# Ordering attention keys beside the scores instead of ahead of them, in blocks of 16 heads

## Chip, core and metric

The kernel runs on one NeuronCore of a Trainium2 chip. The metric is the device time of one execution in microseconds: 10973.53 us, the median of 3 runs (10972.97 to 10985.72). A core has five engines with queues of their own: TensorE (PE in the profile, PEld for its weight loads), VectorE (DVE), ScalarE (ACT), GpSimd (POOL) and SyncE (SP). SP and POOL issue the transfers (DMAs) between HBM and SBUF. Each engine works through its own list in order. An instruction that waits holds up all that stand behind it in that list.

## What is computed

Four layers over a graph of 3327 nodes with 128 features and a dense matrix `adj`; each layer adds its result to `x`. The change concerns the first, an attention with 128 heads of 8 elements each:

```python
q = (x @ Wq.T).reshape(d, n, h)      # d = 128 heads, n = 3327, h = 8
k = (x @ Wk.T).reshape(d, n, h)
v = (x @ Wv.T).reshape(d, n, h)
a = jnp.einsum('dnh,dmh->dnm', q, k) * scale
a = a + spatial_encoding + edge_encoding          # both are adj
a = jax.nn.softmax(a, axis=2)
out = jnp.einsum('dnm,dmh->dnh', a, v)
```

Here `x` is the input after a normalisation and a ReLU. The reshape reads the flat products in a new order: one head is a run of 3327 x 8 numbers of the flat product, so its keys must be put in a new order before they are of use. The three later layers multiply by `adj` or its transpose and are not touched.

## The kernel before, in words

**Preparation (L326 to L436).** Nodes are held as 26 tiles of up to 128. For each pair of tiles PE projects keys and queries. The keys go to HBM as they are (`kraw_d`, one long row per element, in which head d has N numbers from d * N on). Queries are split into a high part, rounded to fp32r, and the rest (`qS_d`). Between them the first four "squares" of `adj` are transposed: `Square` (L264) loads 32 rows at a time as `rows`, DVE turns them in two halves into `cols` (L288) and takes the largest of each row (L292); `store` writes `cols` to `adjT` in pieces of 512 bytes; `gather`, `back` and `finish` take the row maxima through HBM as 4-byte elements, into `bound_d`, the shift of the exponent. Then 13 steps project the values, two tiles each, and store them through two buffers (L427 to L436). In the last eight of these steps `k_halves(e)` (L412) orders the keys of one element for all 128 heads: it loads a row per head from `kraw_d`, splits it into high part (ACT, L420) and rest (DVE, L421), even and odd tiles apart, and makes four stores to `kS_d`. The order of the instructions in the preparation is left to the scheduler of the framework. Behind it stand two branches: a slow path that these inputs don't take (L458), and the main one (L599).

**Attention (L599 to L831).** From here the order is written out by hand. Target nodes go in 7 chunks of 476 columns, in each of them 32 groups of 4 heads, in each group 13 pairs of source tiles. All pairs are numbered through as u. For each pair and head PE adds q.k onto a PSUM bank that DVE has seeded with adj minus the shift (`seed`, L642), ACT takes the exponent (L666, L669), for some banks DVE by a polynomial (`hand_exp`, L685), and PE multiplies by the values into `po` (L713). At the end of a group DVE copies `po` to `OS` (L721), and POOL stores it to `oT_d` (L725).

`loads(u)` (L727) prepares the next group while one is worked on. With q the pair's place in its group: at q = 1 SP issues `load_k` (16 transfers of `KT` from `kS_d`), the first `load_q` and `load_v`; at q = 3, 5, 7 POOL negates the queries just loaded (`negate_q`, L570) and SP issues the next `load_q`, which waits for that negation because both write the same tile; at q = 8 POOL spreads the values (`spread_v`, L580) and copies one column of `KT` to `seen` (`all_here`, L584). The first scores of the next group wait for `seen`.

`plan(u, f)` (L755) puts other work behind pair u: it is issued at that place in every engine's list, ahead of the pair's `loads`. `plan_squares(c)` (L758) spreads the squares of the next chunk over this one: one square over four groups, its rows loaded at a group's first pair, turned at the fifth and tenth, their largest taken at the thirteenth; `gather` stands at the first pair of the fifth group, `back` at its second, `finish` and `store` at its eighth and ninth. The pool `e_t` has one buffer for `rows` and one for `cols`, so a new load waits until the old contents have been used.

```python
            if at == 0 and i >= 0:
                for f, a in behind.pop(i // 4, ()):
                    f(*a)
            if at == 0 and 0 <= i // 4 < n:
                loads(i // 4)
```

## Time and profile before

| what | us |
|---|---|
| median of 3 runs | 10973.53 |
| the profiled execution, its own time | 10981.99 |
| its span, first to last instruction | 10980.2 |
| last eviction of the values ends | 351.4 |
| last subtraction of the keys (DVE, L421) ends | 413.85 |
| first scores | 456.16 |
| `OS` copies of group 0 and of group 32 | 511.55 and 1897.46 |
| PE busy, share of the span | 10536.5, 96% |
| ACT busy | 10031.9, 91% |
| DVE busy | 8481.1, 77% |
| POOL busy | 1532.1, 14% |

The profile is of one execution. In timelines each line has the start in us from the span's beginning, the duration (of all instructions merged in the line), engine, line of the kernel, operation, what it writes and reads, how many, and in brackets how long the engine was idle before and what released it. In the list of waits a line says who waited for whom, for how long in total, how often, and the longest. A busy share of PE counts pipelined matmuls and is no measure of its peak.

### The profile page before, as it was taken

The numbers are of one execution on the slowest core, as the hardware profiler recorded it, in microseconds if no ns is written. First come the engines' busy times: TensorE is split into PE (matmuls) and PEld (weight loads), VectorE is DVE, ScalarE is ACT, GpSimd is POOL, SyncE is SP. The second block draws the span as 40 slices with busy tenths as digits, with TensorE's granted clock in tenths as the row PEclk, the third lists the DMA queues.
The fourth block names the chain that finished last, engine by engine and source line by source line (L and its number), as shares of the span: only waits on it lengthen the run. The fifth ranks groups of instructions, "written<-read, shape, count | busy, mean of one in ns | idle before, by whom it ended". The sixth has DMA issues, their size and how long they took to land. (4 is left out here: it accounts for less than half of the span.)

```text
span 10980.2 us, 204468 instructions
## 1 busy us (share of the span) xinstructions
PE 10536.5 (96%) x72876; PEld 3438.3 (31%) x72876; DVE 8481.1 (77%) x13503; ACT 10031.9 (91%) x13789; POOL 1532.1 (14%) x2480
## 2 busy tenths in 40 slices
PE   4599999999999999999999999999999999999889
PEld 2133333333333333333333323333323333333544
DVE  5588887888878887788887888878877777777655
ACT  3599999999999999999999999999999999999330
POOL 5011111111111111111111111111111111111101
PEclk7799999999999999999999999999999999999999
DMA  8865665665565565565556555565555555554678
GB/s 249 254 99 94 96 96 111 96 97 95 89 119 94 96 97 86 109 99 93 90 95 118 94 96 93 94 118 97 87 92 96 97 94 87 81 88 72 203 235 281
DMA packets 695338, 1256.97 MB, mean 114 GB/s; under 512 B 195218, under 2 KB 555049, under 8 KB 691244
## 3 DMA queue, kind: packets, MB, share of 16 engines
q1 hardware_dynamic: 644044, 1114.42, 55.4%
q0 software_dynamic: 50272, 129.37, 4.3%
q8 instruction: 586, 9.60, 0.4%
q14 instruction: 436, 3.57, 0.1%
HBM read 1096.53 MB, written 146.60 MB: 113 GB/s over the span
## 5 line engine op out<-in xcount | busy, mean ns | idle before, releaser
L666 ACT ACTIVATE e<-S 128x952 f32<-128x952 f32 (+1 forms) x9024 | 8366.0, 1102 | 40.3 <-PE S L654 33.6
L713 PE MATMUL po<-e,VA 128*9 128x476 f32 (+1 forms) x46592 | 5739.3, 565 | 33.1 <-DVE OS L721 12.6
L645 DVE TENSOR_TENSOR S<-a,shb 128x476 f32<-128x476 f32 (+1 forms) x5824 | 3940.7, 677 | 1450.4 <-ACT e L666 1062.5
L654 PE MATMUL S<-QS,KT 64*128 64x476 f32 (+1 forms) x22176 | 4533.8, 445 | 77.8 <-DMA a<-adjT 23.3
L654 PEld LDWEIGHTS S<-QS,KT 64*128 64x128 f32 x22176 | 2077.0, 184 | 5103.7 <-ACT e L666 1281.6
L669 ACT ACTIVATE e<-S 128x476 f32<-128x476 f32 (+1 forms) x4128 | 2476.1, 714 | 24.1 <-PE S L654 23.6
L695 DVE SCALAR_TENSOR_TENSOR e<-e,h 128x476 f32<-128x476 f32 (+1 forms) x2240 | 1493.9, 667 | 77.0
L713 PEld LDWEIGHTS po<-e,VA 128*9 128x9 f32 x46592 | 691.0, 88 | 1606.3 <-issue 1487.9
L570 POOL TENSOR_SCALAR QS<-QS 128x476 fp32r<-128x476 f32 (+1 forms) x669 | 484.8, 725 | 4292.9 <-DMA QS<-qS_d 2457.6
L725 POOL DMA_DIRECT2D oT_d<-OS x896 | 471.9, 532 | 3665.3 <-DVE OS L721 3622.1
L691 DVE TENSOR_SCALAR h<-S 128x476 f32<-128x476 f32 (+1 forms) x1120 | 728.0, 650 | 327.0 <-PE S L654 322.5
L697 DVE SCALAR_TENSOR_TENSOR e<-e,EA 128x476 f32<-128x476 f32 (+1 forms) x1120 | 754.0, 673 | 0.0
L695 DVE SCALAR_TENSOR_TENSOR e<-h 128x476 f32<-128x476 f32 (+1 forms) x1120 | 743.6, 664 | 0.0
L1110 PE MATMUL pu<-strip,y 128*128 128x512 f32 (+2 forms) x1456 | 600.2, 566 | 30.3 <-DVE y L971 14.8
L654 PE MATMUL S<-QZ,KT 64*128 64x476 f32 (+1 forms) x1120 | 494.4, 441 | 10.6 <-DVE S L645 9.3
L1110 PEld LDWEIGHTS pu<-strip,y 128*128 128x128 f32 (+1 forms) x1456 | 271.4, 191 | 304.5 <-issue 271.1
L580 POOL COPY VA<-VR 128x832 f32<-128x832 f32 x224 | 245.6, 1097 | 24.7 <-DMA VR<-v_d 24.7
L1114 DVE TENSOR_REDUCE deg<-strip 128x1 f32<-128x1536 f32 (+1 forms) x104 | 193.7, 1881 | 62.1 <-DMA strip<-adjT 43.5
L654 PEld LDWEIGHTS S<-QZ,KT 64*128 64x128 f32 x1120 | 205.4, 183 | 87.1 <-DVE S L645 47.7
L288 DVE STREAM_TRANSPOSE cols<-rows 128x416 f32<-128x416 f32 x208 | 204.5, 988 | 30.6 <-DMA rows<-in_adj_dram 23.4
L721 DVE COPY OS<-po 128x476 f32<-128x476 f32 (+1 forms) x224 | 146.2, 653 | 88.8 <-PE po L713 88.8
L1063 ACT COPY uT<-pu 128x512 f32<-128x512 f32 (+1 forms) x21 | 11.1, 553 | 222.3 <-PE pu L1110 222.3
(256 smaller groups left out, 1956.7 us busy)
## 6 DMA issues: line engine op xcount, KB each, us to landing
KT<-kS_d SPq DMA_DIRECT2D x1792, 208.0 KB
KT<-kS_d SPq DMA_DIRECT2D x1792, 104.0 KB
VR<-v_d SPq DMA_DIRECT2D x224, 416.0 KB
QS<-qS_d SPq DMA_DIRECT2D x3072, 14.9 KB
QS<-qS_d SPq DMA_DIRECT2D x1536, 29.8 KB
adjT<-cols SPq DMA_DIRECT2D x26, 1664.0 KB
a<-adjT SPq DMA_DIRECT2D x156, 238.0 KB
strip<-adjT POOLq DMA_DIRECT2D x39, 895.5 KB, 5.5
```

The source lines that it names most:

```text
L570: nc.gpsimd.tensor_scalar(QS[b][:, j + 1, :w], QS[b][:, j, :w].bitcast(F32), -1.0, 0.0, op0=ALU.mult, op1=ALU.add)
L580: nc.gpsimd.tensor_copy(VA[(c * NG + g) % 2][:, :, :, 0:H], v.rearrange("p j (t e) -> p t j e", e=H))
L645: touch(u, [r], nc.vector.tensor_tensor(bank(u, r), adj_of[c][2 * q + r][:, :w], shift_of[c][:, :w], op=ALU.subtract))
L654: x = nc.tensor.matmul(bank(u, r), KT[b][64 * r:64 * r + 64, max(0, j - 1), q * P:(q + 1) * P], q_s[64 * r:64 * r + 64, :w], start=hand an ...
L666: touch(u, (0, 1), nc.scalar.activation(e[:, :, :w], S[:, odd:even + 1, :w], AF.Exp, scale=2.0))
L669: touch(u, [r], nc.scalar.activation(e[:, 1 - r, :w], bank(u, r), AF.Exp, scale=2.0))
L691: touch(u, [1], nc.vector.tensor_scalar(s, bank(u, 1), EXP_ARG, None, op0=ALU.mult))
L695: nc.vector.scalar_tensor_tensor(e, s if k == 3 else e, EXP_C[k], s, op0=ALU.add, op1=ALU.mult)
L697: nc.vector.scalar_tensor_tensor(e, e, EXP_C[0], EA[pairs[u][2]][:, :w], op0=ALU.add, op1=ALU.mult)
L713: nc.tensor.matmul(po[32 * j:32 * j + H + 1, :w], VA[k % 2][:, 2 * pairs[v][2] + of, j, :], e_of[v, j][:, 1 - of, :w], start=(q == 0 and r ...
L725: nc.gpsimd.dma_start(oT_d[:, d * N + c * CW:d * N + c * CW + w], o[32 * j:32 * j + H + 1, :w])
L1110: nc.tensor.matmul(ps[:, :k], y[:m, t, :], s[:m, c * 4 * P - c0:c * 4 * P - c0 + k], start=(t == 0), stop=(t == NT - 1))
```

## The change

`k_halves` becomes `k_block(b)`: the 128 partitions now hold 16 heads with 8 elements each instead of 128 heads of one element (`KB` is 16), so eight blocks replace eight elements. Only block 0, of the heads that the first four groups use, is ordered in the preparation, at the third step of the values. Blocks 1 to 7 are planned into the first chunk, each over 52 pairs (four groups), ahead of the four groups that use it.

A block loads its rows at its pair 0 into the `cols` buffer. `high` is a DVE copy of 6 or 7 tiles into the `rows` buffer, stored by SP; `low` is a POOL subtraction in the same buffer, in place, so it waits for the high part's store, and is stored in its turn. There are four such high and low pairs, at 8 and 10, 14 and 17, 23 and 25, 27 and 31. The block's keys are first loaded at pair 40.

Chunk 0 no longer calls `plan_squares`. Its four squares go into blocks 1 to 4, behind the keys: a tighter timetable in pairs 32 to 52, with `gather` and `store` at pair 52, the next block's pair 0, and `back` and `finish` at 58 and 64. The `rows` buffer grows from 832 to 896 columns. The slow path orders blocks 1 to 7 itself. The same numbers are computed as before.

```diff
+KB = P // H
-            self.rows = self.pool.tile([P, KW], F32, name="rows")
+            self.rows = self.pool.tile([P, 7 * P], F32, name="rows")[:, :KW]
+    def k_rows(b):
+        return bass.AP(tensor=kraw_d.tensor, offset=kraw_d.offset + KB * b * N, ap=[[N, KB], [GP, H], [1, N]])
+    def k_store(b, i, r, q0, half):
+        m = half.shape[-1]
+        nc.sync.dma_start(bass.AP(
+            tensor=kS_d.tensor, offset=kS_d.offset + (i * H * HEADS + KB * b) * NP + (r * NQ + q0) * P,
+            ap=[[NP, KB], [HEADS * NP, H], [1, m]]), half)
+    def k_block(b, pool):
...
-            if t0 >= 10:
-                k_halves(t0 // 2 - 5)
+            if t0 == 4:
+                k_block(0, a2)
...
-                if c + 1 < NC and (g, q) == (0, 0):
+                if c and c + 1 < NC and (g, q) == (0, 0):
                     plan_squares(c)
...
+                def load(self):
+                    raw = e_t.tile([P, NT, P], F32, name="cols").rearrange("p t n -> p (t n)")
+                    nc.gpsimd.memset(raw[:, N:NP], 0.0)
+                    nc.sync.dma_start(raw[:, :N], k_rows(self.b))
+                    self.of = raw.rearrange("d (p q r) -> d r q p", q=NQ, r=2)
+                def high(self, r, q0, q1):
+                    self.part = e_t.tile([P, 7 * P], F32, name="rows")[:, :(q1 - q0) * P]
+                    nc.vector.tensor_copy(self.part.rearrange("d (q p) -> d q p", p=P).bitcast(F32R),
+                                          self.of[:, r, q0:q1, :])
+                    k_store(self.b, 0, r, q0, self.part)
+                def low(self, r, q0, q1):
+                    part = self.part.rearrange("d (q p) -> d q p", p=P)
+                    nc.gpsimd.tensor_tensor(part.bitcast(F32R), self.of[:, r, q0:q1, :], part, op=ALU.subtract)
+                    k_store(self.b, 1, r, q0, self.part)
+            def plan_keys():
+                for b in range(1, HEADS // KB):
+                    u, keys = 4 * (b - 1) * NQ, Keys(b)
+                    plan(u, keys.load)
+                    for hi, lo, r, h in ((8, 10, 0, 0), (14, 17, 0, 1), (23, 25, 1, 0), (27, 31, 1, 1)):
+                        plan(u + hi, keys.high, r, 7 * h, 7 + 6 * h)
+                        plan(u + lo, keys.low, r, 7 * h, 7 + 6 * h)
+                    if b <= squares_of(1) - squares_of(0):
+                        sq = Square(e_t, squares_of(0) + b - 1)
+                        for j, (t0, t1, t2) in enumerate(((32, 36, 37), (38, 40, 41), (42, 48, 49), (49, 51, 52))):
+                            plan(u + t0, sq.load, j)
+                            plan(u + t1, sq.turn, j, 0)
+                            plan(u + t2, sq.turn, j, 1)
+                            plan(u + t2, sq.largest, j)
+                        for k, f in ((52, sq.gather), (52, sq.store), (58, sq.back), (64, sq.finish)):
+                            plan(u + k, f)
+            plan_keys()
```

More of the change, by code (lines that the diff above doesn't have):

```diff
@@ L320, in square @@
         return q
+    def k_rows(b):
[6 more added lines that the diff above has]
+    def k_block(b, pool):
+        raw = pool.tile([P, NP], F32, name="st_q0")
+        nc.gpsimd.memset(raw[:, N:NP], 0.0)
+        nc.sync.dma_start(raw[:, :N], k_rows(b))
+        of = raw.rearrange("d (p q r) -> d r q p", q=NQ, r=2)
+        for r in range(2):
+            hi = pool.tile([P, NQ, P], F32R, name="st_k0")
+            lo = pool.tile([P, NQ, P], F32R, name="st_q1")
+            nc.scalar.copy(hi, of[:, r])
+            nc.vector.tensor_tensor(lo, of[:, r], hi.bitcast(F32), op=ALU.subtract)
+            for i, half in enumerate((hi, lo)):
+                k_store(b, i, r, 0, half.bitcast(F32).rearrange("d q p -> d (q p)"))
     def head_rows(tensor):
@@ L410, in bound_scores @@
             return wide
-        def k_halves(e):
-            raw = a2.tile([P, NP], F32, name="st_q0")
-            nc.gpsimd.memset(raw[:, N:NP], 0.0)
-            nc.sync.dma_start(raw[:, :N], head_rows(kraw_d[e]))
-            of = raw.rearrange("d (p q r) -> d r q p", q=NQ, r=2)
-            for r in range(2):
-                hi = a2.tile([P, NQ, P], F32R, name="st_k0")
-                lo = a2.tile([P, NQ, P], F32R, name="st_q1")
-                nc.scalar.copy(hi, of[:, r])
-                nc.vector.tensor_tensor(lo, of[:, r], hi.bitcast(F32), op=ALU.subtract)
-                for i, half in enumerate((hi, lo)):
-                    nc.sync.dma_start(kS_d[i, e, :, r * NQ * P:(r + 1) * NQ * P],
-                                      half.bitcast(F32).rearrange("d q p -> d (q p)"))
         v_rows = v_d.rearrange("(p t) d -> p t d", t=NT)
@@ L460, in gnn_kernel @@
                 square(d2, s, d2)
+            for b in range(1, HEADS // KB):
+                k_block(b, d1)
             for t in range(NT):
@@ L756, in plan, with __init__ @@
                 behind.setdefault(u, []).append((f, a))
+            class Keys:
+                def __init__(self, b):
+                    self.b = b
+                def load(self):
+                    raw = e_t.tile([P, NT, P], F32, name="cols").rearrange("p t n -> p (t n)")
+                    nc.gpsimd.memset(raw[:, N:NP], 0.0)
+                    nc.sync.dma_start(raw[:, :N], k_rows(self.b))
[10 more added lines that the diff above has]
+            def plan_keys():
+                for b in range(1, HEADS // KB):
+                    u, keys = 4 * (b - 1) * NQ, Keys(b)
[12 more added lines that the diff above has]
+                            plan(u + k, f)
             def plan_squares(c):
```

## The prediction

> **What bounds the kernel now.** I read the page's slices first, for where TensorE is not full.
>
> ```profile
> PE   4599999999999999999999999999999999999889
> ACT  3599999999999999999999999999999999999330
> DMA  8865665665565565565556555565555555554678
> ```
>
> Each digit is 274.5 us. Two slices at the start have PE at 4 and 5 with DMA at 8: the preparation. Then PE and ACT stand at 9 with DMA at 5 or 6. So the start is bound by transfers, the middle by PE and ACT together. Second view: windows (columns: stretch, its length, busy us and instructions of PE, PEld, DVE, ACT, POOL, then clock, DMA share, GB/s).
>
> ```profile
> 260.00:415.00 155.00, 57.98 (x131) 25.83 (x131) 78.81 (x62) 67.01 (x43) 7.53 (x19) 0.71 0.92 352
> ...
> 460.00:1860.00 1400.00, 1385.71 (x10041) 424.83 (x10044) 1133.41 (x1744) 1395.36 (x1903) 187.01 (x304) 1.00 0.61 102
> ...
> 141.00:146.00 5.00, 4.55 (x6) 1.99 (x7) 1.50 (x3) 2.07 (x4) 4.34 (x7) 0.52 0.98 289
> ...
> 763.00:776.00 13.00, 12.71 (x94) 3.59 (x93) 11.18 (x18) 12.84 (x18) 2.11 (x4) 1.00 0.99 124
> ```
>
> 260 to 415 us is the values' projection with all eight `k_halves`: DMA is 92% busy, PE a third. 460 to 1860 is the first chunk: DVE has a fifth of its time free and DMA two fifths. The last two lines give prices: storing a square (512-byte pieces) runs at 289 GB/s, so 1664 KB take 5.9 us; loading a group's `KT` (16 copies of each row) runs at only 124 GB/s, so 8 x 208 + 8 x 104 KB take 20.6 us.
>
> Third view: one plain group's loads on POOL and on the SP queue, in order of time.
>
> ```profile
> 784.13 1.08 POOL L570 TENSOR_SCALAR QS<-QS 128x476 fp32r<-128x476 f32 x1 [10.21 <-DMA QS<-qS_d]
> 788.93 0.83 POOL L570 TENSOR_SCALAR QS<-QS 128x476 fp32r<-128x476 f32 x1 [3.72 <-DMA QS<-qS_d]
> 793.56 0.59 POOL L570 TENSOR_SCALAR QS<-QS 128x476 fp32r<-128x476 f32 x1 [3.80 <-PE S L654]
> ...
> 795.34 0.18 POOL L584 COPY seen<-KT 128x3 f32<-128x3 f32 x1
> ```
>
> ```profile
> 673.27 1.75 SPq L299 DMA_DIRECT2D rowmax_d<-rm  x4
> 682.18 0.38 SPq L304 DMA_DIRECT2D four<-rowmax_d  x1
> 682.97 1.35 SPq L551 DMA_DIRECT2D KT<-kS_d  x3
> ...
> 803.17 1.70 SPq L551 DMA_DIRECT2D KT<-kS_d  x4
> ```
>
> A group takes 43.2 us (the `OS` copies stand at 814.02 and 857.24), a pair 3.32. A group's `OS` copy is issued 16 pairs behind its first scores, so those of the group with `OS` at 857.24 came at 804.1; call such a time F. The next group's `KT` is issued at F - 1 (803.17), as soon as the buffer is free. `KT` issue to `seen` took 35.4 us (760.06 to 795.5): 20 us of data, then three rounds of load, negate, load. So `seen` stands at F + 34.5 and the next scores at F + 43.2: the spare time is 8.7 us. The SP lines show how it can go: the 4-byte writes of `gather` took 8.9 us until `four` could be read behind them, `KT` was issued at 682.97 (F + 8.5), `seen` ended at 716.6 and the next F was 717.8. Fourth view, waits: what a late transfer costs.
>
> ```profile
> DVE cols L288 <- DMA rows<-in_adj_dram: 8.9, 1, 8.9
> ...
> PE S L654 <- POOL seen L584: 5.8, 2, 4.3
> ```
>
> The one DVE wait of 8.9 us made its group 53.1 us (`OS` at 8183.34 and 8236.41), 9.9 longer; the PE wait of 4.3 made one 49.3 (5145.21 and 5194.52), 6.1 longer. DVE and PE have no reserve against a late tile beyond a pair or so.
>
> **What the preparation gains.** Seven of eight key loads and 28 of 32 key stores go: 7 x (1664 + 4 x 832) KB = 35.8 MB, at 352 GB/s 102 us if nothing else bound. But the projection stays: 13 steps of two tiles, each 4 evictions and a 1024 KB store. Before, the last eviction (ACT 350.29, 1.07 us) ended at 351.4 and the rest to 413.9 was keys alone: 62.5 us, the lower bound. Up to 351 the steps waited on the store two back (38.8 us of DVE idle there). The third step was at 291.5, held by the first stores beside keys and 4-byte `bound_d` writes; that stays. The other ten took 6.0 us each; PE needs 3.7 (8 records at 0.668 us overlap to 3.70 in the timeline), upper bound 84 us. I take 4.3, since the store's round trip over two buffers stays in the loop: 291.5 + 43 + 1.3 = 336, **78 us** gained. The start-up behind it (414 to first scores at 456) stays.
>
> **What the first chunk pays.** New prices. `high` reads with a stride of 26 elements: L421 reads the same stride at 3333 / 1664 = 2.0 ns per element, L390 contiguously at 1954 / 3328 = 0.59; I take the strided row, 1.5 us for 6 tiles and 1.8 for 7 (low end 0.5). `low`: POOL's two-input add took 1269 / 512 = 2.5 ns, so 1.9 to 2.2 us; strided up to twice that. A 384 or 448 KB store takes 1.2 us at 374 GB/s (the keys' rate at 399 to 412) and I allow 3 us from issue to landing; from 1 (a `QS` load's last issue to its negation) to 8.9 (`gather`). `behind` work of pair p reaches DVE at F + 3.32p + 1.4 (a plain square's `largest` at p = 12: F + 41.1). Seven blocks of four groups A to D:
>
> 1. A, blocks 2 to 5: the square before ends at p = 0. Its last turn and `largest` end at F + 3.4, `gather` issues to 5.2, the store of `cols` follows and needs 5.9 us, behind the 4-byte writes or beside them: landed at F + 12 to 18, I take 15. `Keys.load` uses the same buffer, so SP waits there, and the group's `KT` behind it. 1.7 MB at 374 GB/s come first (4.5 us), so `KT` data start near F + 20 and `seen`, 33 us later, is near F + 53: 10 us late, 11 us paid. Four times: **44** (24 to 60). A DVE wait in the same place (`finish` at p = 12, whose `four` is queued behind those loads) lies beside this.
> 2. B, the same blocks: the high store (p = 8) is queued behind the late `load_q`, the low follows it, and high at p = 14 waits for the row buffer: 3 us x 4 = **12** (0 to 20).
> 3. B, all blocks: at p = 14 SP waits for the copy before it issues `KT`, so `KT` leaves at F + 7 instead of F - 1; `seen` comes 33.6 us later (682.97 to 716.6), F + 41, just in time. But low (p = 17) stands behind `negate_q` and its store behind `load_q`; it lands at F + 36 to 37, high at p = 23 is due at F + 34.6: 2 us x 7 = **14** (0 to 20).
> 4. C, blocks 1 to 4: `KT` leaves at F + 7 again (p = 27), low (p = 31) runs after the first negation at F + 29 (22 us behind `KT`, as 682.97 to 704.89 in the group above), its store lands at 36, only then may the rows of the square (p = 32) come, behind `load_q`: issued 37 to 39, landed 41. The turn at p = 36 is due at F + 34.6: 6.5 us x 4, at the price above **26** (0 to 40).
> 5. The first raw load, 4.5 us, stands ahead of group 1's `KT`, whose `seen` was already late: **4** (0 to 5).
> 6. Inserted work: 28 copies, 28 subtractions and denser turns. DVE is free 0.6 us of each 3.3, a copy takes 1.8; groups with three 1 us operations of a square are at most 0.1 us longer than plain ones. I take 0.4 per copy with its subtraction: **11** (1 to 42).
>
> POOL's subtraction can also hold DVE: at 714.72 the final multiply (L697) took 1.03 us instead of 0.65 while POOL's `VA` copy ran from 715.19; that is in item 6 at its row's price, 0.4. The Trainium skill (SBUF — State Buffer, Who interferes with whom) says a VectorE instruction with two SBUF inputs and a GpSimd instruction that reads SBUF exclude each other for a whole instruction; seeds have two such inputs. By that rule 28 subtractions of about 2.06 us could hold seeds for 58 us, where the row gives 11.
>
> Sum: 44 + 12 + 14 + 26 + 4 + 11 = 111 against 78: **33 us slower**. The profiled execution took 10981.99 us (span 10980.2 and 1.8 around it), 8.5 over the median 10973.53; 11015 by its own clock, 11006.5 beside the median, so 11006.
>
> **Rivals.**
> - It hides (faster): stores of keys and squares land soon enough that items 2 to 4 vanish and item 1 pays 6 us a time. For it: DMA is 39% idle in the chunk, and the SP lines show a square's `gather` wait used up without loss. Against: the order of the SP queue, not bandwidth, sets my delays. It decides where the waits come to under 78 us, a `cols` store landing by F + 12. Price 24 + 4 + 11 = 39, so 39 us faster, 10935; with the gain at 84 and less inserted, 10905.
> - Near balance: half of items 2 to 4 (26) with 44 + 4 + 11 = 85: 10980.
> - The dependence is coarse: `k_store` and `load_k` interleave in one DRAM tensor. If SP waits for each store's landing before the next `KT`, that is 3 us more in B and C of seven blocks, 42 us: 11048. Nothing in this trace has a load of `kS_d` between its stores, so neither way is shown.
> - The preparation doesn't shrink as said: the steps stay at 6 us, the gain 62.5: 11022. Against: the key stores beside them are gone.
>
> **Chances.** Forecast 0.43; coarse 0.10; preparation 0.07; balance 0.17; hidden 0.23. Range 10930 to 11080: hidden beyond 39 us and sums with item 1 at 60 and item 4 at 40 fall outside. Its own range for the forecast: 10996 to 11045. A measurement tells 0.2%, 22 us, from no change: slower 0.58 (forecast, coarse, most of preparation), same 0.19, faster 0.23.
>
> **What would show it.** The projection should end near 336 and first scores near 378. In the waits: PE on `seen` some 10 us four times, ahead of groups 5, 9, 13 and 17; DVE on `rows` in four groups for 6 us; high on its buffer for 2 to 3. Groups of plain chunks must stay at 43.2. If the `OS` copies of the first chunk stay at 43.2 to 44 us throughout, items 1 to 4 are wrong; if the first scores come after 395, the gain is.

## The result, and the profile after

| | us |
|---|---|
| before, median of 4 runs | 10978.91 (10972.97 to 10985.72) |
| after, median of 4 runs | 11112.02 (11105.01 to 11113.34) |
| ratio after to before | 1.0119, 95% interval 1.0106 to 1.0131 |

The change makes the kernel 133 us slower; the forecast was 33 us slower. The two profiled executions differ by 129.5 us in span, and it goes by stretches like this. OS(n) is the start of the copy of group n's output, L733 in after and L721 in before.

| stretch | before | after | difference | forecast |
|---|---|---|---|---|
| start to first scores | 456.2 | 376.3 | -79.8 | -78 |
| first scores to OS(0) | 55.4 | 67.4 | +12.1 | +4 |
| OS(0) to OS(32), first chunk | 1385.9 | 1594.4 | +208.5 | +107 |
| OS(32) to OS(223) | 8275.3 | 8261.6 | -13.7 | 0 |
| rest of the span | 807.5 | 809.8 | +2.4 | 0 |
| sum | 10980.2 | 11109.7 | +129.5 | +33 |

Of the 13.7 us by which the later chunks are shorter, 6.8 lie in the one chunk where before had the late group with PE's wait of 4.3 us; after is not late there. The rest is spread over the other chunks.

The page's slices of after, the same three rows as of before:

```profile
PE   4788899999999999999999999999999999999889
ACT  3587899999999999999999999999999999999430
DMA  8766565656556555565655556565555555554678
```

The second slice rises from 5 to 7, since the preparation ends 80 us earlier. The next three fall from 9 to 8 on PE: that is the first chunk with the keys in it. From the sixth on PE's row is the same. The windows of after (stretch, length, busy us of PE, PEld, DVE, ACT, POOL, then clock, DMA share, GB/s) show the same two places:

```profile
260.00:336.00 76.00, 57.97 (x131) 26.64 (x131) 33.66 (x48) 20.94 (x29) 6.40 (x12) 0.81 0.76 240
443.00:2038.00 1595.00, 1430.99 (x9988) 426.96 (x9984) 1184.46 (x1751) 1391.91 (x1883) 250.81 (x338) 0.94 0.61 108
```

The projection now fits into 260 to 336 us (it ended near 336, as forecast); DMA is busy for 76% of that time, where it was for 92% of 260 to 415 us. In the first chunk PE ran the same work, but its granted clock is 0.94 on average, where before had 1.00. That column had no step in the prediction.

The group differences OS(n) - OS(n-1), against a plain group of 43.2 us:

| groups | excess in after, us | sum | forecast |
|---|---|---|---|
| A behind a square (4, 8, 12, 16) | 27.3, 26.5, 25.3, 25.3 | 104 | 56 (items 1, 2) |
| B (1, 5, ... 25) | 5.3 to 7.7, mean 6.5 | 46 | 14 (item 3) |
| C with a square's turns (2, 6, 10, 14) | 11.1, 10.1, 10.7, 11.7 | 44 | 26 (item 4) |
| A without a square (20, 24) | 3.7, 4.9 | 9 | 0 |
| D (3, 7, 11, 15) | 1.5 each | 6 | 0 |

So 194 of the 209 us stand where the prediction put them, and there they are 1.7 to 3.3 times as large; 15 stand in groups for which it had nothing. (The forecasts of the table are 96 us; the 11 of item 6 were spread over all groups.) Now to what the losses are made of. The waits of the first chunk in after (who <- for whom: total us, times, longest):

```profile
POOL cols L777 <- DMA adjT<-cols: 95.6, 4, 24.3
...
DVE rows L783 <- DMA kS_d<-rows: 54.5, 12, 8.7
DVE b L309 <- DMA four<-rowmax_d: 52.0, 4, 15.4
PE S L666 <- POOL seen L596: 50.2, 5, 14.5
...
DVE cols L289 <- DMA rows<-in_adj_dram: 25.5, 4, 6.5
```

First line: GpSimd at the fill of `cols` ahead of a raw load; it waits for the store of the square's columns. Second: the high half waits for its row buffer, 12 times. Third and fourth: `finish` on its row maxima and PE on the marked keys, in four blocks, at the same time (the fifth wait of PE is another group's). Last: the turns of the squares, 6.4 us four times. The forecast had 10, 3 (and 2) and 6.5 us for these. The SP queue in block 2's A group (first scores near 582.4; start, duration):

```profile
585.88 1.75 SPq L300 DMA_DIRECT2D rowmax_d<-rm  x4
587.68 0.58 SPq L296 DMA_DIRECT2D adjT<-cols  x1
599.63 0.56 SPq L778 DMA_DIRECT2D cols<-kraw_d  x1
600.29 11.92 SPq L563 DMA_DIRECT2D KT<-kS_d  x10
```

The queue stands from 588.3 to 599.6 for the columns' store, then the raw load goes, and only behind it the next group's keys: item 1's mechanism, 17.2 us behind the first scores where 15 were taken. What it costs is seen in windows along the end of this group:

```profile
614.00:627.50 13.50, 12.89 (x95) 3.87 (x95) 8.82 (x14) 12.38 (x18) 0.00 (x0) 1.00 1.03 130
627.50:642.00 14.50, 0.04 (x4) 0.00 (x0) 1.12 (x3) 1.23 (x2) 3.18 (x5) 0.60 0.34 64
642.00:650.00 8.00, 7.92 (x44) 2.37 (x48) 6.52 (x7) 5.11 (x7) 2.64 (x2) 0.66 0.28 67
650.00:653.00 3.00, 3.00 (x23) 0.85 (x15) 0.30 (x1) 3.00 (x6) 0.00 (x0) 1.00 0.61 153
653.00:661.00 8.00, 0.06 (x1) 0.00 (x0) 3.24 (x5) 0.95 (x2) 0.00 (x0) 0.79 0.15 25
661.00:670.00 9.00, 8.98 (x57) 2.46 (x57) 5.95 (x10) 6.71 (x9) 2.13 (x4) 0.81 1.05 163
```

PE stands 14.5 us for `seen`, then works at a clock of 0.66: 44 matmuls in 8 us where the first line has 95 in 13.5. Then it stands 8 us more, while the second high half waits for its buffer (7.4 us by the timeline), and works again at 0.81. Two stands of 22.5 us together and some 4.4 us of work lost at half clock make nearly all of the 27.3.

This adds up over the whole chunk. PE's stands of more than 0.3 us between OS(0) and OS(32) are 153.4 us in after (2.4 in before). The trace's record of the granted clock has 21 stretches at 0.5 that begin in this time, in steps of 3.4 us (3.4 to 17.1), 177.5 us in all; before has none. Half of the part of them that lies outside of the stands is 52.0 us of lost work. 153.4 + 52.0 = 205.4 of the 208.5. **A quarter of the loss is the clock behind the waits, not the waits.** This reckoning says where PE's time went; what made PE stand, it does not say. The Trainium skill (TensorE: Matmul & The Clock Gate, Part 1: The HAM clock gate) says the array falls to half rate after an idle window of about 3.4 us and needs one busy window to come back. The steps of 3.4 us agree. But here shorter stands were followed by half clock as well: all those of 2.4 us or more, such as the 2.8 us from 691.1 to 693.9, and three of the nine of 1.2 to 1.9 us (at 907.6, 1047.1 and 1655.0).

One row stands behind a size that was wrong. The raw load of block 2 in after:

```profile
601.50:608.50 7.00, 7.00 (x56) 2.44 (x52) 5.95 (x10) 7.00 (x10) 0.87 (x2) 1.00 0.98 215
```

and a raw load of one element in before:

```profile
362.00:369.50 7.50, 0.00 (x0) 0.00 (x0) 0.00 (x0) 3.11 (x1) 0.00 (x0) 0.50 1.00 426
```

The same 1.7 MB, the same packets of 13308 bytes, and the DMA engines fully busy in both, but 215 instead of 426 GB/s. A packet takes 1000 ns instead of 498 (medians of the 128 packets of such a load), so the load takes 8 us instead of the 4.5 that I took from before.

### The profile page after: what moved, and what is told of

The parts are those of the page before. It is cut to its first block, busy times and chain, and to the rows that moved or that the text cites. A ratio compares the mean times of both kernels' runs of the same rounds, so it can differ in the third digit from the quotient of the medians.

```text
span 11109.7 us, 204547 instructions
## 1 busy us (share of the span) xinstructions
PE 10591.1 (95%) x72876; PEld 3448.5 (31%) x72876; DVE 8496.4 (76%) x13517; ACT 9995.8 (90%) x13775; POOL 1597.6 (14%) x2508
## 5 line engine op out<-in xcount | busy, mean ns | idle before, releaser
L1163 PE MATMUL pu<-strip,y 128*128 128x512 f32 (+2 forms) x1456 | 599.8, 566 | 30.7 <-DVE y L1024 14.8
L733 DVE COPY OS<-po 128x476 f32<-128x476 f32 (+1 forms) x224 | 146.4, 653 | 96.9 <-PE po L725 96.9
L1116 ACT COPY uT<-pu 128x512 f32<-128x512 f32 (+1 forms) x21 | 11.1, 554 | 222.1 <-PE pu L1163 222.1
```

Of the source, the lines that this page charges most:

```text
L1163: nc.tensor.matmul(ps[:, :k], y[:m, t, :], s[:m, c * 4 * P - c0:c * 4 * P - c0 + k], start=(t == 0), stop=(t == NT - 1))
```

## The experiments

**Theory 1** is the prediction's: the order on SP's queue and the single buffers `cols` and `rows` set the delays. **Theory 2**: the engines hold each other up (GpSimd's subtraction and VectorE share a way to SBUF; more operations). **Theory 3**: the loads of keys depend coarsely on the stores. The trace of after already speaks against it, in two lines of SP's queue:

```profile
658.60 0.54 SPq L329 DMA_DIRECT2D kS_d<-rows  x1
659.24 13.54 SPq L563 DMA_DIRECT2D KT<-kS_d  x16
```

The load of keys is issued 0.1 us after the issue of the store has ended, its first packet (661.43) starts before the store's last one ends (661.82), and nowhere in the chunk does SP's own list of waits have a load of `KT` that waits for a store.

All runs, beside runs of before on the same chip; "stretch" is OS(0) to OS(32) less the 1385.9 of before, "stands" and "clock" are its two parts, worked out as above.

| kernel | time, us | ratio, 95% | first scores | stretch | stands | clock |
|---|---|---|---|---|---|---|
| after | 11112.0 | 1.0106 to 1.0131 | 376.3 | 208.5 | 153.4 | 52.0 |
| finish moved | 11100.1 | 1.0091 to 1.0125 | 374.0 | 196.6 | 137.4 | 58.1 |
| two row buffers | 11066.0 | 1.0060 to 1.0093 | 373.6 | 168.3 | 119.8 | 44.2 |
| no read by GpSimd | 11104.7 | 1.0094 to 1.0128 | 374.7 | 209.5 | 160.4 | 51.4 |
| raw behind keys | 11063.2 | 1.0063 to 1.0094 | 373.6 | 170.4 | 128.5 | 45.3 |
| GpSimd's queue | 11082.7 | 1.0088 to 1.0119 | 372.7 | 175.1 | 127.2 | 44.6 |
| rows by element | 11223.0 | 1.0200 to 1.0234 | 399.7 | 281.0 | 212.8 | 70.5 |
| other pitch | 11117.0 | 1.0111 to 1.0142 | 375.1 | 207.8 | 155.5 | 48.7 |
| eight transfers | 11111.2 | 1.0111 to 1.0142 | 374.9 | 204.2 | 147.1 | 55.7 |
| layout alone | 11012.5 | 1.0022 to 1.0049 | 493.6 | -1.4 | 1.9 | 0 |
| squares in preparation | 11142.4 | 1.0135 to 1.0166 | 526.9 | 84.9 | 52.0 | 30.3 |
| pieces | 11113.0 | 1.0110 to 1.0141 | 524.2 | 62.2 | 45.9 | 16.9 |
| pieces, rows by element | 11142.1 | 1.0141 to 1.0169 | 548.3 | 63.3 | 50.0 | 12.9 |
| new plan, GpSimd | 11061.3 | 1.0057 to 1.0085 | 376.2 | 160.8 | 121.4 | 45.5 |
| new plan, its queue | 11055.6 | 1.0056 to 1.0084 | 376.1 | 136.1 | 88.2 | 44.5 |
| new plan, VectorE | 10992.2 | 1.0004 to 1.0022 | 374.4 | 73.2 | 54.4 | 6.3 |
| new plan, finer | 10990.2 | 1.0000 to 1.0018 | 377.5 | 87.8 | 68.3 | 10.7 |

### What in the order costs how much

**The bounds' writes moved away.**

```diff
-for k, f in ((52, sq.gather), (52, sq.store), (58, sq.back), (64, sq.finish)):
+for k, f in ((52, sq.gather), (52, sq.store)):
+    ...
+plan(16 * NQ + 32 + b, sq.back)
+plan(16 * NQ + 36 + b, sq.finish)
```

> Kernel after, but the last two steps of the four squares of the second chunk (reading the row sums back, and writing the bounds of four bytes each) are planned for a late group of the first chunk, away from the blocks of keys. Theory 1 (the order on the one queue and the single buffers): the second high half of blocks 2 to 5 no longer waits behind the small writes, so its wait falls from 7.4-8.7 us to about 3 in four blocks, about 20 us: some 11092 us. The wait of PE for the negations after each block (14.5 us, four times) stays, since only the finish that lay beside it has gone. Theory 2 (engines hold each other up): the same work is done in another place, so 11112 within 6 us. Theory 3 (dependence of the loads of keys on the stores): 11112 within 6 us, too.

Measured: 11100.1. Its waits in the first chunk:

```profile
DVE rows L783 <- DMA kS_d<-rows: 34.4, 13, 3.5
...
PE S L666 <- POOL seen L596: 45.3, 4, 12.5
...
DVE b L309 <- DMA four<-rowmax_d: 2.3, 2, 1.5
```

The second high half's wait fell from 7.4-8.7 to at most 3.5, and `finish` waits no more, while PE's wait for `seen` stays: `finish` did lie beside it, as item 1 said, and the bounds' write made the 4 to 5 us that item 2 lacked. The trace of after shows how: in block 2 the low half's store had moved its last packet at 652.34, and 13 of its 16 completions came by 652.8, but the last came at 657.57, among those of the bounds' write that was issued behind it at 649.78. In this run the same copy starts 0.5 us behind the store's last packet. The four A groups lost 23.6 us; groups B and others gave half of it back, so 12 us came out of the 20.

**Two row buffers.**

```diff
-self.rows = self.pool.tile([P, 7 * P], F32, name="rows")[:, :KW]
+self.rows = self.pool.tile([P, 7 * P], F32, name="rows", **self.more)[:, :KW]
-self.part = e_t.tile([P, 7 * P], F32, name="rows")[:, :(q1 - q0) * P]
+self.part = e_t.tile([P, 7 * P], F32, name="rows", bufs=2)[:, :(q1 - q0) * P]
...
+Square.more = {"bufs": 2}
```

> Kernel after, but the row buffer that the halves of keys and the rows of the squares share is there twice, so that no half waits for the store before it; to make space two of the 28 buffers of adjacency words are left out, which may cost something at the later chunk boundaries. Read in the first chunk, from the copy of the scores of group 0 to that of group 32: 1594.4 us in after. Theory 1: the waits of DVE and POOL for the store of the rows (54.5 and 46.9 us) and those of the columns' turns (about 26 us) fall to nearly nothing, and the first chunk loses 60 to 90 us, to some 1505-1535; the waits for the raw load ahead of a group's keys stay. Theory 2: the work is the same and lies closer, so the first chunk stays within 20 us of 1594. Theory 3: the stores land earlier, the load of keys waits for less, 10 to 20 us.

Measured: 11066.0, 40 us off the first chunk where 60 to 90 were expected. DVE's wait for the rows (54.5 us) is gone. But the turns still wait 20 us, so those rows are late by their place in the queue and not for the buffer; and GpSimd still waits 61 us for stores, since `low` works in place and waits for its own high's store. So the high halves waited for the single buffer, as theory 1 says; the turns and the low halves did not.

**The raw load behind the keys.**

```diff
-plan(u, keys.load)
-for hi, lo, r, h in ((8, 10, 0, 0), (14, 17, 0, 1), (23, 25, 1, 0), (27, 31, 1, 1)):
+plan(u + 2, keys.load)
+for hi, lo, r, h in ((12, 14, 0, 0), (17, 20, 0, 1), (24, 26, 1, 0), (28, 32, 1, 1)):
```

> Kernel after, with the raw load of a block planned two pairs later, so that it is issued behind the next group's keys instead of ahead of them, and the halves three to four pairs later in the first group, one pair later in the second. Nothing else is moved; the squares keep their places. Theory 1: the keys of the next group no longer wait for the store of the columns and the raw load, so the groups with a square's tail fall from 25-27 us above a quiet group to 5-10 (what stays is the small writes), 60 us or more in four groups, and the groups without a tail by their 4 us; the first high half may wait for the raw data by some us, in seven groups, up to 35 us back. So 11040 to 11090. Theory 2 (engines) and theory 3 (the dependence on the stores): no change, 11106 to 11118, or slower, since the halves come later.

Measured: 11063.2, inside. The A groups behind a square fell from 25-27 to 10.3-15.5 us over plain; the B groups behind them rose to 10.7-14.3, since the high halves came later. In block 2's A group the next group's keys are now issued 6 us behind the first scores (at 575.81; OS(3) is at 580.5), where after needed 18. Yet this group still stands:

```profile
DVE b L309 <- DMA four<-rowmax_d: 10.7, 1, 10.7
PEld S L666 <- POOL seen L596: 10.3, 1, 10.3
```

Both waits are there, each 4 to 5 us shorter: the keys are still behind `gather` and the store, and `finish` still waits for row maxima that are read behind the keys.

**Loads and stores of the keys on GpSimd's queue.**

```diff
-nc.sync.dma_start(raw[:, :N], k_rows(self.b))
+nc.gpsimd.dma_start(raw[:, :N], k_rows(self.b))
-k_store(self.b, 0, r, q0, self.part)
+k_store(self.b, 0, r, q0, self.part, nc.gpsimd)
```

(and the low half's store alike)

> Kernel after, with the raw load of a block and the stores of its halves issued by GpSimd on its own queue instead of SyncE's. Nothing else is moved: each waits for the same buffers. Theory 1: the keys of the next group are no longer issued behind the raw load's wait for the columns' store (12 us), so the groups with a square's tail (25-27 us over a quiet group) lose 10 us or more each; but GpSimd now stands in that wait itself, and its negations and the mark that the keys are there come behind it, so part of it stays: 11060 to 11105. Theory 2 and theory 3: no change, 11112 within 8 us, or slower by GpSimd's 28 stores and 7 loads.

Measured: 11082.7, inside, 29 us gained. PE's wait for `seen` is gone, but the A groups keep 23.9 to 26.8 us: now the first high half stands 11.8 us for the raw load (last completion at 611.35, copy at 611.45 in block 2), whose packets take 1235 to 1366 ns (medians) beside the keys' load, and PE 13.2 us behind it. So with the buffers and the transfers as they are, another order is worth 33 to 38 us of the 208.

### The raw load's half rate

**Rows by element.**

```diff
-ap=[[N, KB], [GP, H], [1, N]]
+ap=[[GP, H], [N, KB], [1, N]]
-ap=[[NP, KB], [HEADS * NP, H], [1, m]]
+ap=[[HEADS * NP, H], [NP, KB], [1, m]]
```

> Kernel after, with the rows of a block taken in the other order: element by element, 16 neighbouring heads after each other, instead of head by head with a jump of 1.7 MB from each row to the next. The same bytes, the same number of packets, and the same halves. Where the raw load's packets of 13308 bytes take 1000 ns in after (498 ns in before): if the order of the rows sets this, they fall to about 500 ns and the load of 1.7 MB from 9 to 4.5 us; by theory 1 this then shortens the wait ahead of a group's keys by 4.5 us in each of six blocks, about 27 us, to some 11085. If it is something else (the buffer, the other transfers), the packets stay at 1000 ns and the time at 11112 within 6 us. The stores, whose order changes too, may be dearer by up to 2 us each.

Measured: 11223.0, 111 us more. The packets stay at 1000 ns, and only eight are in flight at a time where after has 16, so the load takes 18 us:

```profile
637.50:654.00 16.50, 11.54 (x85) 3.47 (x83) 8.97 (x15) 12.25 (x16) 0.52 (x2) 0.99 0.73 134
```

I had not expected the split over eight engines. It makes the run a dose: a load 10 us longer made the A groups behind a square 10.4 to 14.8 us longer, those without one 6.7 and 7.1, and the first scores 23 us later. But the order of the stores changed in the same way, and their data takes 4.1 us instead of 2.0 (medians), so this is a dose of both: that the raw load's length is paid nearly in full is likely, not shown.

**Another pitch, and eight transfers.**

```diff
-GP = GN + 4 * P
+GP = GN + 5 * P + 16
```

> Kernel after, with the pitch from element to element of the raw keys (and of the other arrays of that length) 576 bytes longer: 1,706,048 instead of 1,705,472 bytes. If the packets of 13308 bytes take 1000 ns since rows at this pitch fall on the same part of the memory, they get faster (to 500-700 ns) and the time falls by up to 27 us; if it is another cause, the packets stay at 1000 ns and the time at 11112 within 6 us.

```diff
-nc.sync.dma_start(raw[:, :N], k_rows(self.b))
+for e in range(H):
+    nc.sync.dma_start(raw[e:P:H, :N], bass.AP(tensor=kraw_d.tensor, offset=kraw_d.offset + e * GP + KB * self.b * N,
+                                              ap=[[N, KB], [1, N]]))
```

> Kernel after, with the raw load of a block of the first chunk cut into eight, one for each element, of 16 neighbouring rows each: same rows to same partitions. If the 1000 ns of a 13308-byte packet come from one transfer that goes through eight far parts of the memory, they fall to about 500 ns and the load to some 5-6 us with its eight issues (0.4 us each); the time 11085 to 11110. If they come from something else, the packets stay at 1000 ns and the time is 11112 or up to 15 us more for the eight issues.

Measured: 11117.0 and 11111.2; 219 and 226 GB/s in the raw load. Neither a pitch 576 bytes longer nor eight transfers in place of one changed the rate. Other pitches were not tried, so the cause stays open.

**The layout alone, in before.**

```diff
-nc.sync.dma_start(raw[:, :N], head_rows(kraw_d[e]))
+nc.sync.dma_start(raw[:, :N], bass.AP(tensor=kraw_d.tensor, offset=kraw_d.offset + KB * e * N,
+                                      ap=[[N, KB], [GP, H], [1, N]]))
```

(and the stores alike)

> Kernel before, with all eight blocks of keys still in the preparation, but in blocks of 16 heads and 8 elements as in after, instead of one element and 128 heads. Only the layout changes. If the rows' order makes the packets of 13308 bytes take 1000 ns, the eight loads take 36 us more together; since they lie beside the value steps with their buffers for two, between nothing and 36 us comes out: 10975 to 11015. If the 1000 ns come from what else runs in after, the time stays at 10979 within 6 us and the packets at 500 ns.

Measured: 11012.5; the first scores come 37.4 us later, 4.7 us for each of eight loads with its stores, and the first chunk is that of before. The loads run at 205 GB/s here too (383 to 399 us, packets of 1008 ns in the median). So nothing else that runs in after makes the half rate: the layout of the rows does.

### Engines

**No read by GpSimd: fills in place of its subtraction.**

```diff
-nc.gpsimd.tensor_tensor(part.bitcast(F32R), self.of[:, r, q0:q1, :], part, op=ALU.subtract)
+for _ in range(3):
+    nc.gpsimd.memset(part, 0.0)
```

> Kernel after, with GpSimd's subtraction (2.6 us, reads two operands from SBUF) replaced by three fills of the same buffer, of about the same length together, which read nothing. It leaves out the low half of the keys, so the scores are those of the high half alone, in blocks 2 to 8. Theory 1: nothing waits for GpSimd's reads as such; 11112 within 10 us. Theory 2 (GpSimd's reads keep DVE and the others off SBUF): DVE's work beside them gets quicker, and of the 28 subtractions of 2.6 us, 73 us in all, up to that much goes: 11040-11090.

Measured: 11104.7, the first chunk 1595.4 against 1594.4 in after. GpSimd's reads, the first half of theory 2, fall as the cause in this plan; that there are more operations was not changed here. Yet the mechanism is real: VectorE's seeds that lie beside a subtraction take 1620 ns on average in after (22 in the first chunk) and 719 beside the fills. All seeds of the window 600 to 1250 us together have a mean of 699 ns in after and of 670 here:

```profile
L657 DVE TENSOR_TENSOR S<-a,shb 128x476 f32<-128x476 f32 x310 | 207.5, 670 | 71.5 <-ACT e L678 54.3 <-ACT e L681 3.4 <-PE S L666 0.5
```

VectorE was held, but the chunk did not get shorter without it; that a transfer set the end of those groups is the likely reason.

### Can the gain be kept?

**The squares in the preparation**, between the values' steps (the core of the diff):

```diff
+if t0 >= 6 and t0 % 6 == 0:
+    more.append(square(a_t, squares_of(0) + t0 // 6 - 1, a1))
+    more[-1].gather()
...
-if b <= squares_of(1) - squares_of(0):
+if False:
```

> Kernel after, with the four squares of the second chunk made in the preparation, between the value steps, instead of between the blocks of keys. Theory 1: the groups with a square's tail (27.3, 26.5, 25.3 and 25.3 us over a quiet group) fall to the 4.3 us of the groups without one; the groups with the squares' turns (43.6 us in all) to a fourth; the second high halves lose some 20 us: the stretch from the scores of group 0 to those of group 32 goes from 1594.4 to about 1440-1465 us. The preparation gets longer by what four squares cost there, which nothing in the trace of after shows: between nothing (the value steps wait for loads) and 60 us. So 10965 to 11020 us. Theory 2 (engines): the stretch loses only the squares' own DVE time, four times 5 us or so. Theory 3 (the load of keys waits for the whole store): 20 to 40 us.

Measured: 11142.4. The first chunk did nearly what theory 1 says (1470.8 where 1440 to 1465 were expected, so the squares' part in after is 124 us), but the preparation took 150 us more, 38 a square, where at most 60 in all were expected. Its window:

```profile
380.00:520.00 140.00, 13.06 (x16) 5.15 (x16) 29.18 (x41) 1.88 (x2) 5.94 (x16) 0.50 0.46 92
```

The busiest engine works for a fifth of it and the DMA engines for half: loads of rows and turns follow each other through one buffer.

**Pieces**, on top of it: six parts instead of four, in two halves of one buffer by turns, two to a group.

```diff
-for hi, lo, r, h in ((8, 10, 0, 0), (14, 17, 0, 1), (23, 25, 1, 0), (27, 31, 1, 1)):
+for k in range(6):
+    v = u + NQ * (k // 2) + k % 2 + (0 if u or k > 1 else 3)
+    plan(v + 8, keys.high, k)
+    plan(v + (10 if u or k > 1 else 9), keys.low, k)
```

> Kernel after, with the four squares in the preparation as in the run before, and with the halves of the keys in three pieces (5, 4 and 4 tiles) instead of two, in two parts of one row buffer by turns: two pieces in each of the block's first three groups, high at the pairs 8 and 9, low at 10 and 11, so that each store has a group's length before its buffer is wanted again. One of 28 buffers of adjacency words is left out for it. Theory 1: the waits for the rows' stores go (B groups 45.7 us and C groups' rest), what stays is the start, about 10 us, and 4 to 9 us in the groups with a raw load: from group 0 to group 32 about 1400-1425 us against 1385.9 in before, and the time 10930 to 10990, by what the squares cost in the preparation. Theory 2: the same number of elements is copied and subtracted, so the stretch is no better than in the run before less 10 us.

> The kernel of the run before (squares in the preparation, keys in three pieces and two parts of a buffer), with the rows of a block element by element, 16 neighbouring heads after each other. Theory 1 with the rows' order as the cause of the slow raw load: its packets fall from 1000 to about 500 ns, the group with the raw load has no wait left, and the time is 10 to 30 us under the run before: 10910 to 10970. If the order is not the cause: the same as the run before within 6 us.

Measured: 11113.0 and 11142.1. The stretch fell by 23 us more (1448.1; expected 1400 to 1425), but GpSimd still waited 56.5 us for stores, in place as before. The second of the two again pays 24 us in the preparation for its slower raw load.

**A new plan.** Blocks in three groups instead of four, squares behind the last block from group 20 or 21 on, nothing in the window where SP issues the keys' loads. Four runs, each to mend what the trace of the last one showed:

```diff
+u, keys = (3 * b - 2) * NQ, Keys(b)
+plan(u - (4 if b > 1 else 11), keys.load)
+for k, at in enumerate((0, 9, 11, 13, 22, 24)):
+    plan(u + at, keys.piece, k)          # high and low on GpSimd, into two parts of the buffer
```

> Kernel after, with another plan of the same blocks: both halves of a piece on GpSimd (3 pieces per parity of 5, 4 and 4 tiles), the high half in one part and the low half in another part of a row buffer of ten tiles, so that no low half waits for a store; pieces at the pairs 0, 9 and 11, outside of the issue of the keys' loads; a block's raw load at pair 9 of the group before, behind the keys' loads instead of ahead; a block in three groups, and the four squares from group 21 to 30, their loads at the pairs 0 and 9 too. One of 28 buffers of adjacency words is left out. Theory 1 (the order on the one queue and the single buffers): with every transfer outside of the keys' window the stretch from the scores of group 0 to those of group 32 falls from 1594.4 to 1395-1430 us (1385.9 in before), the gain of the preparation (80 us) stays, and the time is 10910 to 10950, under before. Theory 2 (engines): GpSimd now has 19 us more per block and DVE the squares in half the groups, so 40 us or more stay above 1430. Theory 3: the stores are done groups ahead, as by theory 1.

Measured: 11061.3, missed by 110. Two waits of my own making: at pair 0 GpSimd stood 11 us for the raw load six times, with SP's keys behind its store; and `finish` four pairs behind `gather` held DVE 39 us in four groups.

```diff
+for k, at in enumerate((9, 11, 14, 22, 24, 27)):
+    plan(u + at, keys.piece, k)          # raw load and stores on GpSimd's queue
+for k, f in ((26, sq.store), (26, sq.gather), (30, sq.back), (39, sq.finish)):
```

> The plan of the run with both halves on GpSimd, mended where its trace showed waits: the raw load and the stores of the halves on GpSimd's own queue instead of the one that loads the keys; no piece at pair 0 (there GpSimd waited 11 us for the raw load and SyncE's loads of keys waited behind the store); pieces at the pairs 9, 11 and 1 in three groups; the four squares from group 20 on, two loads at once in a row buffer of 13 tiles, the writes of the bounds 13 pairs after the gather instead of 4. Two of 28 buffers of adjacency words are left out. Theory 1: the groups with keys lose their 46.4-57.9 us and come to 43.2-45; the groups with a square's end (52-61 us) to 44-47; from group 0 to group 32 about 1395-1430 us (1546.7 in the run before, 1385.9 in the kernel before); the time 10915 to 10955. Theory 2 (the work itself, on whichever engine): the stretch stays above 1500.

Measured: 11055.6, missed again. Most groups with pieces take 48 to 51 us, though hardly anything waits there for a transfer (GpSimd for stores, 20 us in 29 times). The timeline of VectorE:

```profile
600.03 0.64 DVE L711 SCALAR_TENSOR_TENSOR e<-h 128x476 f32<-128x476 f32 x1
600.71 4.67 DVE L711 SCALAR_TENSOR_TENSOR e<-e,h 128x476 f32<-128x476 f32 x2
605.30 2.20 DVE L661 TENSOR_TENSOR S<-a,shb 128x476 f32<-128x476 f32 x2
```

and of GpSimd in the same kernel:

```profile
600.10 1.90 POOL L793 CAST rows<-cols 128x640 fp32r<-128x640 f32 x1
602.30 0.61 POOL L333 DMA_DIRECT2D kS_d<-rows  x1 [0.30 <-POOL rows L793]
602.93 1.93 POOL L795 TENSOR_TENSOR rows<-cols,rows 128x640 fp32r<-128x640 f32 x1
```

Two VectorE operations of 0.65 us each took 4.67 us together, as long as GpSimd's copy and subtraction beside them. This is the rule that the prediction weighed and priced low: here, with few transfers left to hide it, it looks like the bound. The next run takes these reads off GpSimd, and makes the pieces smaller as well:

```diff
-nc.gpsimd.tensor_copy(by_q[0].bitcast(F32R), of)
+nc.vector.tensor_copy(by_q.bitcast(F32R), of)
-nc.gpsimd.tensor_tensor(by_q[1].bitcast(F32R), of, by_q[0], op=ALU.subtract)
+nc.vector.tensor_tensor(by_q.bitcast(F32R), of, self.part(k, 0)[3], op=ALU.subtract)
+at = (9, 11, 12, 14, 16, 17, 19, 21, 22, 24, 25, 27, 29, 30, 32, 34)
```

> The plan of the run before, with both halves of the keys on VectorE in pieces of 3 or 4 tiles (8 pieces, 16 operations of 0.5 to 1.1 us for a block, about 12 us in three groups, in which VectorE is idle 7 us each), one operation in a pair without an exponential by hand; two parts of the row buffer by turns, the stores still on GpSimd's queue, and the rows of the squares too. The trace of the run before shows VectorE's operations of 0.67 us taking 1.4 to 1.8 us on average beside GpSimd's copies and subtractions, and 43.2 us where GpSimd has no piece. If GpSimd's reads beside VectorE are what is left of the price in that plan: the groups with keys come from 48-51 to 43.2-46 us, the stretch from group 0 to group 32 to 1410-1450, and the time to 10935-10975. If the work itself or the transfers cost: the stretch stays at 1500 or more.

Measured: 10992.2, 120 us below after, 0.13% over before. The groups with keys are at 43.9 to 46.0, and the clock stands at 0.99:

```profile
432.00:1892.00 1460.00, 1391.10 (x9994) 412.85 (x9994) 1217.34 (x1838) 1393.61 (x1884) 286.23 (x494) 0.99 0.65 118
```

VectorE has 95 us more to do here than in before's chunk (1122.67 us from 511 to 1898) and the chunk is 73 us longer: 37 us in the 20 groups with keys, about 1.9 each, and the rest in the squares' groups. So most of the price of the run before went with GpSimd's reads or with the size of the pieces; the two were not tried apart. At the later chunk boundaries 26 buffers of adjacency words cost 2 to 5 us each.

```diff
+at = [NQ * g + q for g in range(3) for q in (1, 3, 4, 6, 8, 9, 11, 12)][:20]   # ten pieces, 12 tiles, 27 buffers
```

> The plan of the run before, finer: ten pieces of 2 or 3 tiles for a block, 20 operations of VectorE of at most 0.8 us spread over all three groups; a row buffer of 12 tiles, so that 27 of the 28 buffers of adjacency words stay (the run before, with 26, took 2 to 5 us more at each later chunk boundary than the kernel after, 24 us in five); the rows of the squares loaded one at a time by GpSimd, with three to four pairs before VectorE turns them (in the run before VectorE stood 6.6 and 4.1 us before two turns). If the rest of the price is in these waits: the groups with keys 43.5-45 us (44.2-46.0 in the run before), the stretch from group 0 to group 32 1415-1445 us, the later chunks 8265-8275 us, the time 10935-10970, below before. If the elements' work itself costs its 2 us in each group: the stretch stays at 1450-1465 and the time is 10970-10985, the same as before.

Measured: 10990.2, ratio 1.0000 to 1.0018: no gain. The later chunks came back to 8275.6 us as expected, the groups with keys stayed at 44.3 to 45.7 (one, the second, had 54.8: VectorE stood 8.1 us for block 2's raw load), and the squares got dearer. As far as these two runs show, the work itself, in small pieces and nearly without waits for transfers, costs about what the preparation gains. None of the 16 kernels beats before.

## Why the prediction was right in sign and wrong in size

- **What bounds the kernel, and the gain**: right. 79.8 us to the first scores against 78, with the last eviction at 336.4 against 336.
- **Item 1, the A groups**: right place and mechanism, the SP lines show it. PE's four stands for the keys are 9.9 to 14.5 us, 49 in all, where 10 each were taken. Two rows were too small: the raw load was priced at before's rate (4.5 us) and took 8, and the columns' store ended at 17 instead of 15 us.
- **Item 2, the second high half**: 3 us taken, 7.4 to 8.7 measured, and 36 us of PE's stands in four groups where 12 were forecast. The step "3 us from issue to landing" failed: the store's last completions come among those of the four-byte bounds of `finish`, which I had counted only as lying beside the late keys. Moving them took the wait to 3.5 at most.
- **Item 3, the B groups**: 2 us taken, 6.5 measured. In block 2 the high half waits 2.2 us and PE stands 2.8 (691.1 to 693.9): the wait is the forecast's. Behind it come 3.4 us at half clock. Over the seven groups the stands are 22 us and the work lost at half clock 23, which together are nearly the 46: here the clock is the larger half of the loss.
- **Item 4, the C groups**: the turn's wait of 6.5 us was measured at 6.3 to 6.5. What was missing is again the clock: each stand of 6 us had 6.8 to 10.2 us at 0.5.
- **The term that no step had**: 52 us at half clock. My two rows for "what a late transfer costs" (8.9 us made 9.9, 4.3 made 6.1) held it already for one long stand (the mean clock of those two groups was 0.90 and 0.93), and item 1 used it so; but items 2 to 5 were summed wait by wait at one for one. For many stands of 3 to 8 us, each of which brings 3.4 us or more at half clock, that fails. Of the 101 us by which the first chunk passed its forecast (208.5 against 107), 52 are this term and 24 are item 2.
- **Item 5**: 4 taken; 12.1 in this profile, 5.6 to 12.1 in six other kernels that keep the first load in its place and its layout.
- **Item 6 and the rule of the port**: the time did not depend on it in after, so 11 was no worse than 58. The rule's mechanism is there, and in a plan with few queue waits it probably decides: taking the reads off GpSimd there, with smaller pieces, brought 63 us.
- **Rivals**: "hides" found no support: even in a plan with nearly all waits for transfers gone, the chunk gave back 73 us. "Coarse dependence" is refuted by SP's queue: `KT` is issued right behind a store, without a wait for its landing. "The preparation doesn't shrink" is refuted.

What stays open: why packets of this layout take 1000 ns (far larger changes of the pitch were not tried), and why some stands under 2 us bring the half clock and others do not.

## What to carry to other kernels

Price a stand of TensorE with the half clock behind it: in after each stand of 2.4 us or more cost itself and 1.7 to 3.3 us on top. Take a transfer's rate only from a row with the same access pattern; the same bytes in the same packets ran at half rate in another order of rows. Before moving work beside a stage in which two engines are at 99%, count its busy time on the third: 12 us of VectorE a block, finely spread, came back as 5 us of time in the groups with keys and, with the squares pushed together behind them, as 10, where the preparation had given 11.

## What the hardware showed beyond the expected

- The granted clock falls to 0.5 in steps of 3.4 us behind all stands of 2.4 us or more in after, and behind some as short as 1.4 us.
- 13308-byte packets at 498 ns (128 rows of one element) and 1000 ns (16 heads by 8 elements), with both pitches tried, in either order of rows and in one transfer or eight; eight in flight instead of 16 when the outer count is eight.
- VectorE's strided copy of an even number of tiles is 1.6 to 1.7 times as fast per element: 0.92 us for six tiles and 1.86 for seven in after, 0.68 for four and 1.40 for five in the pieces.
- A 448 KB store with four-byte writes issued behind it had moved its last packet at 652.34 us and completed at 657.57 (block 2 of after); in the run without those writes the copy that waits for the store starts 0.5 us behind its last packet.
- VectorE's operations with two SBUF operands took as long as a GpSimd copy or subtraction beside them: 4.67 us for two of 0.65 us.
